# Rows of experts 1 to 7 gathered as column strips and transposed by VectorE, and the first x by ScalarE's queue

## The chip, the cores and the metric

One core of one Trainium2 chip. The metric is device time in microseconds (us) of one execution: the median of three runs of the kernel before is 932.55 us (932.34 to 934.09). Tensors are fp32. TensorE (PE) multiplies, VectorE (DVE) and ScalarE (ACT) work on SBUF and PSUM, GpSimd (POOL) issues the indirect DMAs (gathers and scatters through a list of row numbers), and SyncE (SP) issues most of the plain DMAs.

## What is computed

```python
xc = einsum('bsd,bdh->bsh', x, W[cat_ids]) + b[cat_ids][:, None, :]   # x: (4, 1024, 512)
xf = xc.reshape(4096, 512)
probs = softmax(xf @ Wr); eidx = argmax(probs)                        # 8 experts
rank = position of the token among those of its expert
keep = rank < 512                                                     # capacity 512
xe = xf[dispatch]                                                     # (8, 512, 512)
h = maximum(einsum('ecd,edf->ecf', xe, W1), 0)                        # F = 2048
ye = einsum('ecf,efd->ecd', h, W2) * (p_tok of the token, 0 if not kept)
out = x + scatter-add of ye to its tokens
```

Four batches each pick one of 64 weight matrices, a router sends each token to one expert, each expert takes at most 512 tokens, and a two-layer ReLU network of the expert is added to x.

## The kernel before

**First stage (0 to about 147 us): the conditional linear layer and the router.** x is loaded in eight chunks of 512 tokens (`load_x`, L245; the first in four DMAs), and each chunk is turned on TensorE against an identity (`transpose_x`, L265, PSUM to SBUF by ScalarE at L274). Every large product in this kernel is done in seven block products in place of eight, with sums and differences of blocks made by VectorE beforehand; `linear` (L470) issues one of the seven at L488 and evicts with VectorE (`finish`, L516; `plus_bias`, L501), and `done` (L509) stores a 256 KB piece of the result into DRAM, in two tensors `xc0_dram` and `xc1_dram` that hold the left and the right 256 columns of each token. Rank and expert give each token a slot; `rank` (L441) scatters (probability, token number) into the DRAM table `slots` with eight indirect DMAs for each batch (L460). `load_w1` (L174) loads the 1 MB of expert weights of one group g of the hidden units, as two halves of 512 KB (L179), and `sum_w1` makes their sums.

**Junction.** ScalarE's queue reads `slots` back as `table` (L637), GpSimd turns it into `src_row` and `dst_row` (L644), the row numbers that gathers and scatters use.

**Experts (from about 147 us, some 96 us each).** `gather` (L682) issues the indirect DMAs at L691. For expert e, `xg` (four buffers of 128 tokens x 512) takes the rows of `xc0_dram` and `xc1_dram`, eight gathers of 1 KB rows; `xr` (four buffers) takes the rows of x, the residual, four gathers of 2 KB rows. `fetch(e)` (L698) copies 8 columns of `src_row` into a tile `at` by VectorE, and then issues both: the residual of expert e and the rows of expert e+1. It is called from `between` at g = 1 and held behind VectorE's latest work. `transpose_rows` (L707) turns a tile of 128 tokens on TensorE (L719: four transposes of 128x128), evicts it into `xe` (L720; VectorE for expert 0, else ScalarE), and behind the last tile VectorE makes the block sums of `xe` (L729 to L733). `first_layer` (L740) issues the products at L746 and evicts into `h`; `second_layer` (L795) the products at L803, `inner_product` (L851) those at L856, where four of the seven second-layer products are themselves split in seven, with their blocks' sums from `inner_sums` (L815, at L160 to L170). `add` (L787) multiplies a result by the probability and adds it onto the residual rows (L791), and four scatters (L889) write these to the output. x itself is copied to the output by three DMAs from DRAM to DRAM (L920).

**Order.** TensorE and SP run in the order of the program (`manual_schedule`). VectorE, ScalarE and GpSimd are put in order by a planner when the kernel is built: what is ready, by place in the program, with `high_priority` ahead. The stretch that ends an expert is the part of the program around the change:

```python
            second_layer(e, 6)
            inner_sums(e, 5)
            ahead(0)
            small(*[(2, q) for q in (1, 5, 2, 6, 3, 7)])
            ahead(1, 2)
            small((2, 4))
            inner_sums(e, 3)
            second_layer(e, 7)
            inner_sums(e, 4)
            small((5, 5), (5, 2))
            ahead(3)
            small(...)
```

`ahead(c)` is `transpose_rows(e + 1, c)`. PSUM results of `first_layer`, `second_layer` and `inner_product` share two buffers each of three tags x, y, z.

Of the kernel before, what the change touches and what calls it, by code (L numbers as in the profile page):

```python
# [8 lines left out]
F32 = mybir.dt.float32  # L9
I32 = mybir.dt.int32  # L10
AF = mybir.ActivationFunctionType
ALU = mybir.AluOpType
# [4 lines left out]
P = 128  # L17

FAR = 8192.0
# [3 lines left out]
def kernel(  # L23
# [11 lines left out]
    nc = tc.nc  # L35
    B, S, D = x.shape
    NCAT = cond_w.shape[0]
    E, _, F = w1.shape
    T = B * S
    CAP = -(-T // E)  # L40
    KC = D // P
# [4 lines left out]
    HT = CT // 2  # L46
    SC = CAP // P
    HK = KC // 2
# [3 lines left out]
    NG = F // (2 * HB * P)  # L52
    W1G = 3
    NS = E * SC
    Q = 32
    ROW = 2
    xf = x.rearrange("b s d -> (b s) d")
# [7 lines left out]
    def keep_warm(pool, n):  # L65

        ps = pool.tile([P, D], F32, tag="t", name="ps_idle")
        for _ in range(n):
            nc.tensor.matmul(ps, lhsT=idle[:, 0:P], rhs=idle, start=True, stop=True)
# [13 lines left out]
    def unordered(group, ins):  # L83
# [10 lines left out]
    nc.vector.memset(idle, 0.0)  # L94
    wr_sb = const.tile([P, KC, Q], F32, name="wr_sb")
    nc.vector.memset(wr_sb, 0.0)
    nc.scalar.dma_start(
        out=wr_sb[:, :, 0:E], in_=wr.rearrange("(kc p) e -> p kc e", p=P)
    )
    zeros = const.tile([P, T * ROW // P], F32, name="zeros")  # L100
    nc.vector.memset(zeros, 0.0)
    slots = dram.tile([T, ROW], F32, name="slots")
    nc.scalar.dma_start(out=slots.rearrange("(p s) r -> p (s r)", p=P), in_=zeros)
    before = const.tile([P, P], F32, name="before")
    make_upper_triangular(nc, before, diag=False)
    ones = const.tile([P, P], F32, name="ones")
# [22 lines left out]
        nc.vector.memset(t, 0.0)  # L129


    xc_dram = [dram.tile([T, HD], F32, name=f"xc{j}_dram") for j in range(2)]

    table = const.tile([P, SC, E, ROW], F32, name="table")
    src_row = const.tile([P, NS], I32, name="src_row")
    dst_row = const.tile([P, NS], I32, name="dst_row")


# [35 lines left out]
    def load_w1(e, g):  # L174

        t = w1p.tile([P, 7, HK, HB * P], F32, tag="w1", name=f"w1_{e}_{g}")
        for half in range(2):
            f = half * F // 2 + g * HB * P
            nc.sync.dma_start(  # L179
                out=t[:, 2 * half : 2 * half + 2, :, :].rearrange("p a k f -> p (a k) f"),  # L180
                in_=w1[e, :, f : f + HB * P].rearrange("(k p) f -> p k f", p=P),
            )
        w1s[e, g] = t

    def sum_w1(e, g):
# [3 lines left out]
    with (  # L189
# [52 lines left out]
            nc.vector.tensor_tensor(t3, b22, b12, ALU.subtract)  # L242
            nc.vector.tensor_tensor(t4, b21, t2, ALU.subtract)

        def load_x(c):  # L245
            t = xin.tile([P, XT, D], F32, tag="x", name=f"x_{c}")
            n = 1 if c == 0 else XT
            for j in range(0, XT, n):
                nc.sync.dma_start(
                    out=t[:, j : j + n, :],  # L250
                    in_=xf[c * CT + j * P : c * CT + (j + n) * P, :].rearrange(
                        "(j p) d -> p j d", p=P
                    ),
                )
            xrows[c] = t
# [214 lines left out]
        def linear(b, g, k):  # L470
# [15 lines left out]
            for j in range(2):  # L486
                for kc in range(HK):
# [10 lines left out]
                        skip_group_check=True,  # L498
                    )

            def plus_bias(into, half):  # L501
                return nc.vector.tensor_tensor(
                    into,
                    ps,
                    bias[:, half * HD : (half + 1) * HD].unsqueeze(1).to_broadcast([P, 2, HD]),
                    ALU.add,
                )

            def done(t, i, j):  # L509
                at = c * CT + i * HT  # L510
                nc.sync.dma_start(
                    out=xc_dram[j][at : at + HT, :].rearrange("(j p) d -> p j d", p=P),
                    in_=t,
                )

            def finish():  # L516
                if k in (1, 6, 7):
                    if (b, k) == (LATE, 6):
                        banks[key, k] = late["all"][:, g, :].rearrange("p (j d) -> p j d", d=HD)
                    else:  # L520
                        banks[key, k] = parts.tile(
                            [P, 2, HD], F32, tag=f"s{k}", bufs=2, name=f"s{k}_{b}_{g}"
                        )
                    evicted = plus_bias(banks[key, k], 0 if k == 1 else 1)
                    if k == 1:
                        latest[0] = evicted
                if k in (2, 3):
                    t = banks.pop((key, 1 if k == 2 else 6))
                    latest[0] = nc.vector.tensor_tensor(t, ps, t, ALU.add)
                    done(t, 0, int(k == 3))  # L530
                if k == (7 if b < B - 1 else 5):
                    t = banks.pop((key, 7))
                    nc.vector.tensor_tensor(t, banks[key, "y"], t, ALU.add)
                    done(t, 1, 1)
                    if b == LATE:
                        t = banks[key, 6]
                        nc.vector.tensor_tensor(t, banks[key, "y"], t, ALU.add)
                if k == 4:
                    t = parts.tile([P, 2, HD], F32, tag="c", bufs=2, name=f"xc10_{c}")
                    plus_bias(t, 0)  # L540
                    done(t, 1, 0)
# [77 lines left out]
        }  # L619

        with tc.manual_schedule(engines={mybir.EngineType.PE, mybir.EngineType.SP}):
            load_x(0)
            load_batch(0)
            load_x(1)
            load_batch(1)
            load_x(2)
            load_batch(2)
            keep_warm(ps_t, 3)
            for i in range(XT):
                transpose_x(0, i)  # L630
            for b in range(B):
                for i, product in enumerate(ORDERS[b]):
                    linear(*(b, *product)[-3:])
                    for f, *at in loads.get((b, i), []) + beside.get((b, i), []):
                        f(*at)
# [20 lines left out]
    ps_p = ctx.enter_context(tc.tile_pool(name="ps_p", bufs=2, space=PSUM, reuse_waits="tile"))  # L656

    rows, residual, xes, hs = {}, {}, {}, {}

    def load_w2(e, when=None):  # L660

# [20 lines left out]
    def gather(e, pool, sources, into, at):  # L682

        n = D // len(sources)
        for j, source in enumerate(sources):
            for c in range(SC):
# [8 lines left out]
                    in_offset=bass.IndirectOffsetOnAxis(ap=at[:, c : c + 1], axis=0),  # L695
                )

    def fetch(e):  # L698

        at = rowp.tile([P, 2 * SC], I32, tag="at", name=f"at_{e}")  # L700
        n = min(2 * SC, NS - e * SC)
        nc.vector.tensor_copy(at[:, 0:n], src_row[:, e * SC : e * SC + n])  # L702
        gather(e, xr, [xf], residual, at[:, 0:SC])
        if e + 1 < E:
            gather(e + 1, xg, xc_dram, rows, at[:, SC : 2 * SC])

    def transpose_rows(e, c, parts=range(2)):  # L707

        if e not in xes:
            xes[e] = xep.tile([P, 7, HK, HC * P], F32, tag="xe", name=f"xe_{e}")  # L710

        t = xes[e]
        r = rows[e * SC + c]
        half, at = divmod(c, HC)
        n = len(parts)
        lo = parts[0] * HK
        ps = ps_e.tile([P, KC, P], F32, tag="t", name=f"ps_e_{e}_{c}_{lo}")
        for kc in range(n * HK):
            nc.tensor.transpose(ps[:, kc, :], r[:, (lo + kc) * P : (lo + kc + 1) * P], ident)  # L719
        (nc.vector.tensor_copy if e == 0 else nc.scalar.copy)(  # L720
            t[
                :, 2 * half + parts[0] : 2 * half + parts[0] + n, :, at * P : (at + 1) * P
            ].rearrange("p b k n -> p (b k) n"),
            ps[:, 0 : n * HK, :],
        )
        if c == SC - 1:
            b11, b21, b12, b22, t1, t2, t4 = (t[:, k, :, :] for k in range(7))
            if 0 in parts:
                nc.vector.tensor_tensor(t1, b12, b11, ALU.subtract)  # L729
            if 1 in parts:  # L730
                nc.vector.tensor_tensor(t2, b22, t1, ALU.subtract)
                nc.vector.tensor_tensor(b12, b22, b12, ALU.subtract)
                nc.vector.tensor_tensor(t4, b21, t2, ALU.subtract)  # L733


    LEFT = {1: 0, 2: 1, 3: 6, 4: 3, 5: 4, 6: 5, 7: 2}
# [184 lines left out]

    with tc.manual_schedule(engines={mybir.EngineType.PE, mybir.EngineType.SP}):
        gather(0, xg, xc_dram, rows, src_row)

        for part, half, then in (
            ([0], 0, [(0, 1)]),
            ([0], 1, [(1, 1), (0, 5), (1, 5)]),
            ([1], 0, [(0, 2)]),
            ([1], 1, [(1, 2)]),
        ):  # L930
            for c in range(half * HC, (half + 1) * HC):
                transpose_rows(0, c, part)
            for g, k in then:
                first_layer(0, g, k)

        load_w2(0, xes[0][:, 3, 0, HC * P - 1 :])
        for e in range(E):
            for g in range(NG):
                if e == 0 and g < 2:
# [21 lines left out]
                for k, q in turns:  # L961
                    inner_product(e, k, q)

            def ahead(*tiles):
                for c in tiles:
                    if e + 1 < E:
                        transpose_rows(e + 1, c)

            second_layer(e, 6)
            inner_sums(e, 5)  # L970
            ahead(0)
            small(*[(2, q) for q in (1, 5, 2, 6, 3, 7)])
            ahead(1, 2)
            small((2, 4))
            inner_sums(e, 3)
            second_layer(e, 7)
            inner_sums(e, 4)
            small((5, 5), (5, 2))
            ahead(3)
            small(  # L980
                *[(5, 1), (5, 3), (5, 6), (3, 5), (5, 7), (3, 2), (5, 4), (3, 1)],
                *[(4, 5), (4, 1), (3, 6), (4, 2), (4, 6)],
# [35 lines left out]
```

## Time and profile before

| what | value |
|---|---|
| three runs, us | 934.09, 932.34, 932.55 |
| the profiled execution's own time, us | 930.86 |
| its span in the profile, us | 929.1 |
| granted TensorE clock | 0.998 |
| DMA | 123.32 MB, mean 133 GB/s |
| gathers of 1 KB rows (L691) | 64 of 0.96 to 1.04 us |
| gathers of residual rows (L691) | 32 of 1.41 us |
| transposes of expert rows (L719) | 128 of 273 ns |

A line of the timeline or of the groups names engine, line of the kernel, operation, and out<-in by the program's names. In the timeline the first number is the start and the second the time from the first start to the last end, both in us, and a bracket tells how long the engine had been idle and what ended that. PEld is the weight load ahead of a product. Matmuls overlap, so the distance from one group's start to the next is their price, not their duration.

### The profile page before, as it was taken

To read this page: it belongs to the slowest core of one execution; us is meant where nothing else is said; L and a number is where in the kernel's file an instruction comes from. 1 tells how busy PE (TensorE), PEld (TensorE's weight loads), DVE (VectorE), ACT (ScalarE), POOL (GpSimd) and SP (SyncE) were. 2 spreads that over 40 slices of the span, in tenths; PEclk is the share of its full clock that TensorE was granted. 3 is DMA by queue.
4 is the path that set the end of the run, shared out by engine and by line. 5 is a ranking of instruction groups with operands and counts; after the bars stand their busy time and mean duration, and the time that the engine had idled before them with its cause. 6 is when DMAs were issued, how large, how long until landed. Compare 5 with 4: busy or idle time off the path is not lost.

```text
span 929.1 us, 13272 instructions
## 1 busy us (share of the span) xinstructions
PE 915.9 (99%) x5318; PEld 817.5 (88%) x5318; DVE 654.9 (70%) x1222; ACT 193.5 (21%) x350; POOL 181.7 (20%) x173
## 2 busy tenths in 40 slices
PE   9999999999999999999999999999999999999996
PEld 6788787889988998899889988999889988998886
DVE  4656684589549954987488847883789368945793
ACT  3323200321132103210331023112311132113200
POOL 0043443060141013201230024001500150012001
PEclk9999999999999999999999999999999999999999
DMA  8475223992372118310841085106520562044001
GB/s 299 157 242 167 81 80 117 343 379 90 100 254 100 46 61 266 127 47 21 275 152 46 1 277 164 58 1 227 182 91 2 202 202 90 2 154 159 1 1 46
DMA packets 95727, 123.32 MB, mean 133 GB/s; under 512 B 8516, under 2 KB 83268, under 8 KB 95474
## 3 DMA queue, kind: packets, MB, share of 16 engines
q1 hardware_dynamic: 85634, 97.54, 31.5%
q0 software_dynamic: 9216, 24.85, 8.1%
q8 instruction: 42, 0.69, 0.3%
q10 hardware_dynamic: 816, 0.08, 0.1%
q14 instruction: 19, 0.16, 0.1%
HBM read 105.96 MB, written 25.23 MB: 141 GB/s over the span
## 4 chain that ended last, share of the span: by engine, by line
PE 64%; issue 18%; DVE 13%; POOL 3%; DMA 1%; ACT 0%; POOLq 0%; DVEq 0%
PE hx L746 19%; PE hy L746 9%; PE yx L856 7%; PE xcx_lin L488 6%; PE hz L746 5%; PE yx L803 4%; PE yy L856 3%; DVE rows L791 2%; PE xcy_lin L488 2%; POOL rows L691 2%; DVE h L160 2%; DVE h L161 2%; PE ps_xT L273 1%; PE xcz_lin L488 1%; DVE h L163 1%
## 5 line engine op out<-in xcount | busy, mean ns | idle before, releaser
L746 PE MATMUL hx<-xe,w 128*128 128x256 f32 x1024 | 237.7, 379 | 1.2 <-DVE xe L720 1.0
L746 PEld LDWEIGHTS hx<-xe,w 128*128 128x128 f32 x1024 | 193.8, 190 | 27.7 <-DVE xe L720 1.2
L889 POOL DMA_INDIRECT out_dram<-rows,dst_row x32 | 32.0, 999 | 465.3 <-DVE rows L791 428.6
L746 PE MATMUL hy<-xe,w 128*128 128x256 f32 x512 | 120.6, 379 | 0.0
L803 PE MATMUL yx<-w_b,h 128*128 128x256 f32 x512 | 113.1, 379 | 0.0
L746 PEld LDWEIGHTS hy<-xe,w 128*128 128x128 f32 x512 | 97.3, 190 | 13.2
L803 PEld LDWEIGHTS yx<-w_b,h 128*128 128x128 f32 x512 | 96.7, 190 | 12.8
L761 ACT COPY s<-hx 128x512 f32<-128x512 f32 x96 | 55.8, 582 | 222.7 <-PE hx L746 222.7
L765 DVE TENSOR_TENSOR h<-hy,s 128x512 f32<-128x512 f32 x64 | 44.1, 688 | 76.0 <-PE hy L746 51.7
L766 ACT ACTIVATE h<-h 128x512 f32<-128x512 f32 x96 | 60.5, 630 | 150.7 <-DVE h L765 150.7
L856 PE MATMUL yx<-w_b,h 128*128 128x128 f32 x640 | 83.4, 275 | 0.7 <-DVE rows L791 0.6
L791 DVE SCALAR_TENSOR_TENSOR rows<-yx,table,rows 128x128 f32<-128x128 f32 (+1 forms) x160 | 59.9, 398 | 30.8 <-PE yx L856 30.7
L856 PEld LDWEIGHTS yx<-w_b,h 128*128 128x128 f32 x640 | 77.3, 192 | 1.1 <-DVE rows L791 1.0
L691 POOL DMA_INDIRECT rows<-in_x_dram,at x32 | 45.2, 1412 | 145.4 <-DVE at L702 106.2
L691 POOL DMA_INDIRECT rows<-xc_dram,at x56 | 58.4, 1043 | 21.4 <-issue 14.3
L746 PE MATMUL hz<-xe,w 128*128 128x256 f32 x256 | 60.6, 379 | 0.6 <-DVE xe L720 0.6
L765 DVE TENSOR_TENSOR h<-hz,s 128x512 f32<-128x512 f32 x32 | 22.0, 688 | 55.4 <-PE hz L746 55.4
L803 PE MATMUL yx<-w_t,h 128*128 128x256 f32 x256 | 56.6, 379 | 0.0
L460 POOL DMA_INDIRECT slots<-row,dest x32 | 36.3, 1136 | 96.4 <-DVE dest L456 87.9
L746 PEld LDWEIGHTS hz<-xe,w 128*128 128x128 f32 x256 | 48.5, 190 | 7.4 <-DVE xe L720 0.9
L803 PEld LDWEIGHTS yx<-w_t,h 128*128 128x128 f32 x256 | 48.6, 190 | 6.6
L856 PE MATMUL yx<-w_t,h 128*128 128x128 f32 x384 | 52.1, 279 | 0.4
(160 smaller groups left out, 1244.3 us busy)
## 6 DMA issues: line engine op xcount, KB each, us to landing
w<-in_L_ffn_W_dram SPq DMA_DIRECT2D x64, 512.0 KB, 4.3
w_b<-in_L_ffn_W_dram SPq DMA_DIRECT2D x32, 1024.0 KB, 10.9
x<-in_x_dram SPq DMA_DIRECT2D x7, 1024.0 KB, 8.7
xc_dram<-s SPq DMA_DIRECT2D x22, 256.0 KB, 2.7
out_dram<-in_x_dram SPq DMA_DIRECT2D x2, 2816.0 KB, 20.3
cw<-in_L_cond_W_dram SPq DMA_DIRECT2D x3, 1024.0 KB, 10.6
out_dram<-in_x_dram SPq DMA_DIRECT2D x1, 2560.0 KB, 12.2
xc_dram<-xc SPq DMA_DIRECT2D x8, 256.0 KB, 2.3
```

Of the source, the lines that this page charges most:

```text
L160: eng.tensor_tensor(s1, a21, a22, ALU.add)
L460: nc.gpsimd.indirect_dma_start(out=slots, out_offset=bass.IndirectOffsetOnAxis(ap=dest[:, j : j + 1], axis=0), in_=row[:, j, :], in_offset ...
L488: nc.tensor.matmul(ps[:, j, :], lhsT=left[:, kc, j * P : (j + 1) * P], rhs=right[k][:, kc, :], start=((k in OPENS or (b, k) == (LATE, 3)) ...
L691: nc.gpsimd.indirect_dma_start(out=into[e * SC + c][:, j * n : (j + 1) * n], out_offset=None, in_=source, in_offset=bass.IndirectOffsetOnA ...
L746: nc.tensor.matmul(ps[:, j, :], lhsT=w1s[e, g][:, LEFT[k], kc, j * P : (j + 1) * P], rhs=xes[e][:, RIGHT1[k], kc, :], start=(k in OPENS an ...
L761: nc.scalar.copy(banks[key, k], ps)
L765: latest[0] = nc.vector.tensor_tensor(into, ps, part, ALU.add)
L766: nc.scalar.activation(into, into, AF.Relu)
L791: nc.vector.scalar_tensor_tensor(row, ps, table[:, half * HC + at, e, 0:1], row, ALU.mult, ALU.add)
L803: nc.tensor.matmul(ps[:, at, :], lhsT=hs[e][:, m // HB, LEFT[k], m % HB, at * P : (at + 1) * P], rhs=w2s[e][RIGHT2[k]][:, m, :], start=(k ...
L856: nc.tensor.matmul(ps, lhsT=left[:, g, :], rhs=right[:, g, :], start=(q in OPENS and g == 0), stop=(q == LAST[BANK[q]] and g == NG - 1), s ...
L889: nc.gpsimd.indirect_dma_start(out=of, out_offset=bass.IndirectOffsetOnAxis(ap=dst_row[:, n : n + 1], axis=0), in_=residual.pop(n), in_off ...
```

## The change

- `done` stores each row of 256 columns as four strips of 64 in another order of columns: strip b holds the columns 32b to 32b+31 of the first 128 and those of the second. The evictions write their tile in that order (`strip`, `bank_of`); the stored pieces become 256 bytes.
- For experts 1 to 7 `gather_strips` reads strips in place of rows: 32 gathers of 128 strips of 256 bytes for each expert, the partition block b of the target taking strip b of 32 tokens. The strip numbers are made once, by four loads of `slots` on ScalarE's queue and eight GpSimd operations (`strip_rows`), and read in place. `turn_strips` turns a 128x512 tile on VectorE in blocks of 32x32, straight into `xe`. The strips of expert 1 are asked for ahead of the loop over experts, those of e+2 when e+1 has been turned. `fetch` keeps the residual alone.
- Expert 0 keeps its gathers and its transposes on TensorE; since its columns come in the new order, its first-layer weights are loaded in that order of rows, 16 DMAs for each g in place of 2.
- The first chunk of x is issued by ScalarE's queue, and the router weights' load and the clearing of `slots` behind it; `keep_warm` multiplies twice in place of three times.

```diff
+    strip_at = const.tile([P, 1], F32, name="strip_at")
+    for b in range(VB):
+        nc.gpsimd.memset(strip_at[b * V : (b + 1) * V, :], float(b))
...
+            into = t[:, 2 * half : 2 * half + 2, :, :]
+            if e > 0:
...
+            rows_of = w1[e, :, f : f + HB * P].rearrange(
+                "(a k q b c) f -> b k c a q f", a=2, k=HK, b=2, c=V
+            )
+            for b in range(2):
+                for k in range(HK):
+                    lo = (b * HK + k) * V
+                    for a in range(2):
+                        nc.sync.dma_start(out=into[lo : lo + V, a], in_=rows_of[b, k, :, a])
...
+            def strip(t):
+                return t.rearrange("p j d -> p (j d)").rearrange(
+                    "p (b j k c) -> p j k b c", b=VB, j=2, c=V
+                )
+
+            def bank_of(t):
+                return t.rearrange("p j (k b c) -> p j k b c", b=VB, c=V)
...
+                return nc.vector.tensor_tensor(strip(into), bank_of(ps), bank_of(added), ALU.add)
...
-                    out=xc_dram[j][at : at + HT, :].rearrange("(j p) d -> p j d", p=P),
-                    in_=t,
+                    out=xc_dram[j][at : at + HT, :].rearrange(
+                        "(j p) (b d) -> p b j d", p=P, b=VB
+                    ),
...
-            load_x(0)
+            load_x(0, nc.scalar)
             load_batch(0)
+            nc.scalar.dma_start(
+                out=wr_sb[:, :, 0:E], in_=wr.rearrange("(kc p) e -> p kc e", p=P)
+            )
+            nc.scalar.dma_start(out=slots.rearrange("(p s) r -> p (s r)", p=P), in_=zeros)
...
-            keep_warm(ps_t, 3)
+            keep_warm(ps_t, 2)
...
+    def strip_rows():
+        for b in range(VB):
+            nc.scalar.dma_start(
+                out=strips[b * V : (b + 1) * V].rearrange("r a c e w -> r a (c e w)"),
+                in_=slots.rearrange("(a r s) w -> r a (s w)", a=VB, r=V),
+            )
+        into = src_strip.rearrange("p e (c a) -> p e c a", a=VB)
+        for a in range(VB):
+            row = strips[:, a, :, :, 1].rearrange("p c e -> p e c")
+            nc.gpsimd.tensor_scalar(row, row, FAR, float(T - 1), ALU.add, ALU.min)
+            nc.gpsimd.tensor_scalar(
+                into[:, :, :, a], row, float(VB), strip_at, ALU.mult, ALU.add
+            )
...
+    def gather_strips(e):
+        at = src_strip[:, e, :]
+        for half in range(2):
+            for j in range(2):
+                t = xg.tile([P, D], F32, tag="rows", name=f"strips_{e}_{half}_{j}")
+                n = D // (HC * VB)
+                for q in range(HC * VB):
+                    c = half * HC * VB + q
+                    nc.gpsimd.indirect_dma_start(
+                        out=t[:, q * n : (q + 1) * n],
+                        out_offset=None,
+                        in_=xc_dram[j].rearrange("t (b d) -> (t b) d", b=VB),
+                        in_offset=bass.IndirectOffsetOnAxis(ap=at[:, c : c + 1], axis=0),
+                    )
+                rows[e, half, j] = t
...
+        at = rowp.tile([P, SC], I32, tag="at", name=f"at_{e}")
+        nc.vector.tensor_copy(at, src_row[:, e * SC : (e + 1) * SC])
+        gather(e, xr, [xf], residual, at)
...
+    def turn_strips(e, half, j):
+        t = rows.pop((e, half, j)).rearrange("p (q k c) -> p k q c", k=HK, c=V)
+        into = xe_of(e)[:, 2 * half + j, :, :].rearrange("p k (q r) -> p k q r", r=V)
+        nc.vector.transpose(into, t)
...
         gather(0, xg, xc_dram, rows, src_row)
+        strip_rows()
...
         load_w2(0, xes[0][:, 3, 0, HC * P - 1 :])
+        gather_strips(1)
         for e in range(E):
...
-            ahead(0)
             small(*[(2, q) for q in (1, 5, 2, 6, 3, 7)])
-            ahead(1, 2)
+            if e + 1 < E:
+                for half in range(2):
+                    for j in range(2):
+                        turn_strips(e + 1, half, j)
+            if e + 2 < E:
+                gather_strips(e + 2)
             small((2, 4))
...
-            ahead(3)
+            if e + 1 < E:
+                sum_xe(e + 1)
```

## The prediction

> **What bounds the kernel now.** I read the page first: its span, its busy shares and the shares of the chain that ended last.
>
> ```profile
> span 929.1 us, 13272 instructions
> ...
> PE 915.9 (99%) x5318; PEld 817.5 (88%) x5318; DVE 654.9 (70%) x1222; ACT 193.5 (21%) x350; POOL 181.7 (20%) x173
> ...
> PE 64%; issue 18%; DVE 13%; POOL 3%; DMA 1%; ACT 0%; POOLq 0%; DVEq 0%
> ```
>
> TensorE is busy for 99% at a granted clock of 9 in all 40 slices. The kernel is as long as TensorE's list of work plus its few waits, so each part is priced by what it takes from that list and by which wait it adds. Then the timeline of the stretch that ends expert 1, for the transposes (L719), the next product (L856) and VectorE's sums beside them:
>
> ```profile
> 316.37 1.04 PE L719 MATMUL ps_e<-ident,rows 128*128 128x128 f32 x8
> 316.61 0.34 DVE L791 SCALAR_TENSOR_TENSOR rows<-yx,table,rows 128x128 f32<-128x128 f32 x1
> 316.87 0.68 DVE L170 TENSOR_TENSOR w_t<-w_t,w_t 128x512 f32<-128x512 f32 x1
> ...
> 317.24 1.06 PE L856 MATMUL yx<-w_b,h 128*128 128x128 f32 x8
> 317.47 0.68 DVE L160 TENSOR_TENSOR h<-h 128x512 f32<-128x512 f32 x1
> 318.07 0.68 DVE L167 TENSOR_TENSOR w_b<-w_b 128x512 f32<-128x512 f32 x1
> ...
> 326.82 0.60 PE L719 MATMUL ps_e<-ident,rows 128*128 128x128 f32 x4
> ...
> 327.26 1.06 PE L856 MATMUL yx<-w_t,h 128*128 128x128 f32 x8
> ...
> 330.25 1.06 PE L856 MATMUL yy<-w_b,h 128*128 128x128 f32 x8
> ```
>
> The transposes' price is the distance to the next product (317.24 - 316.37 = 0.87 for eight), not their mean of 273 ns, which overlaps. VectorE runs back to back here, but ahead of need: the first sums for product k=3 (L160, L167) end at 318.75, and TensorE uses them at 330.25.
>
> Last, the same view around expert 0's first corner sum, where VectorE, GpSimd and TensorE meet:
>
> ```profile
> 174.20 0.92 SPq L179 DMA_DIRECT2D w<-in_L_ffn_W_dram  x2
> ...
> 189.77 3.23 POOL L691 DMA_INDIRECT rows<-in_x_dram,at  x1 [0.30 <-issue]
> ...
> 190.97 1.21 DVE L168 TENSOR_TENSOR w_t<-w_b,w_t 128x1024 f32<-128x1024 f32 x1
> ...
> 196.78 1.02 POOL L691 DMA_INDIRECT rows<-in_x_dram,at  x1 [0.30 <-issue]
> ...
> 203.74 0.87 DVE L791 SCALAR_TENSOR_TENSOR rows<-yx,table,rows 128x256 f32<-128x256 f32 x2
> ...
> 206.82 7.07 PE L803 MATMUL yx<-w_t,h 128*128 128x256 f32 x32
> ```
>
> The gathers of the residual rows run from 187.7 to 197.8. The adds at 203.74 need two of those four tiles, and free the PSUM buffer that the product at 206.82 writes (its weights load from 206.60). There are 2.0 us between the adds' end (204.6) and that.
>
> **A. TensorE's transposes go.** Per expert: 0.43 (310.57 to 311.00) + 0.87 + 0.44 = 1.74 us of pure TensorE time. Seven experts: -12.2. Expert 0's end also loses a wait for gathered rows (213.72 to 214.80 for four, 1.08 in place of 0.43): -0.65. ScalarE's 28 copies (15.7 us) hid beside TensorE: 0.
>
> **B. VectorE's transposes come:** 28 of 128x512, absent from this trace. Nearest row: a two-input sum of that size, 0.68 us, one each 0.60 when back to back. The Trainium skill's page VectorE: DVE Perf Modes, in "Rules for kernel authors", speaks against the change: a 128x128 transpose belongs on TensorE, VectorE having 32x32 blocks alone. Its section "The three transpose paths" gives 311 ns for 128 bf16 columns; with 1.05 ns a column, the slope of L791 (348 ns for 128, 482 for 256), I estimate 311 + 384 x 1.05 = 714 ns for 512. By that rule a block costs 0.18 against TensorE's 0.11 (0.44 / 4), a loss; by the trace the 0.11 is on the bound and the 0.18 is not. Four take 2.4 to 2.9 us; k=3's sums then end near 321.5 against 330.25 - 1.74 = 328.5. Left is the wait of single evictions behind a longer backlog; before, one such wait of 0.24 us per expert shows (L81). I take 0.15 more for each of seven: +1.0 (bounds 0 and +8; a gain is excluded, since VectorE only gets work). If the cover went, all 2.9 x 7 = 20 us would show.
>
> **C. GpSimd's list.** Eight gathers of 1 KB rows per expert (L691, 1043 ns) become 32 of 256-byte strips. A gather has 128 indices either way; the scatters of 8-byte rows (L460) take 1136 ns, so the size of a row hardly counts and I keep 0.95 + 0.30 between two = 1.25 us clear, 40 us per expert of 96. From expert 1 on they run ahead of need, from about 222 on expert 0's clock; the four scatters (245 to 250) and the next residual gathers (266 to 272) wait behind them, to about 270 and 284; the adds come at 300. Cost 0; cover 15 us.
>
> Expert 0 is different. Its 32 gathers for expert 1 start when its own rows are transposed (about 157) and stand ahead of `fetch(0)` in the program, which I take for GpSimd's order. From 157 to 178 VectorE is mostly idle: 16 gathers at 1.27. From 178 to 200.8 VectorE is back to back. The skill's page SBUF — State Buffer, section "SBUF: two separate sides", says that a GpSimd operation that reads SBUF (here its indices) and a VectorE operation with two SBUF inputs exclude each other for a whole instruction. The row above agrees: the 3.23 us gather ends 0.9 after VectorE's next one-SBUF-input operation (192.11). By the rule taken strictly each gather costs 3.2 + 0.3 there. By the rows, the 14 gathers that ran in such stretches average 1.49 + 0.30 = 1.79; I take that: 13 more, 29 by 200.8, all 32 by 204.6, the second residual gather issued by 207.3. Its packets then share the DMA engines with the third out-copy (packets of 45 KB, 1.7 us each in the packet records), which before landed at 192.6 + 19.3 = 211.9. The strips move the same bytes as the old gathers, only earlier, so I keep that end: rows at 212.0, between 207.3 + 3 and 206.0 + 10.7 (what gathers at 203 to 206 took to land). Adds end at 212.9 where 206.6 was needed: **+6.3** (bounds 0 and +18). Behind the adds on VectorE stand the inner sums, but they shift with TensorE.
>
> **D. Start.** The warm-up ends about 1.8 us earlier (6 passes in 5.49 us become 4), x no longer holds SP until 2.95, so `cond_w` (3.99) and the bias behind it go about 1.0 earlier; ScalarE issues x from about 0.7 in place of 1.14, and its two loads that follow are needed late. The first product (9.44) could gain 1.7, but the bias, awaited at 12.18 (L502), gains only SP's 1.0 and holds VectorE's next sums, and with them the third product. -1.0 (bounds -1.7 and +0.5, if the two rings share badly).
>
> **E. Stores and the junction.** 32 stores go from 1 KB to 256-byte pieces. Packet records: 46 ns for 1 KB, 18 ns for 256 bytes, so 64 x 18 - 16 x 46 = +0.4 us of DMA each. They hide except the last: the second half's gathers wait for it (5.42 us to 151.21), and the rows' cover there is 1 us or less. +0.7 (bounds 0 and +2.5). GpSimd's eight small index operations (0.36 us for the like, L644) fit in that 5.42 us wait; after it they'd delay the strips by 3.
>
> **F. SP.** 16 issues for each of four w1 tiles, near 0.45 us (four x issues in 1.81), 7.2 in place of 1.07. In the first stage stores move by up to 4 us; their buffers are double and nobody waits: 0 (bounds 0 and +1). At 174.2 the out-copies move 6 us later, counted in C. The strided evictions keep their size (0.69): 0 (to +1).
>
> **Sum:** -12.2 - 0.65 + 1.0 + 6.3 - 1.0 + 0.7 = -5.85. The profiled execution took 930.86 us, span 929.1 plus 1.8 around it, and becomes 925.0. It lay 1.7 below the median of 932.55, to which I apply the same difference: **926.7**.
>
> **The rivals.** *The residual rows come much later (slower).* Place: GpSimd, 178 to 200.8. At the strict 3.5 us only 6 or 7 gathers fit, the 32 end near 212.7, the second residual gather at 215.4, its rows at 218 to 226. With 222 the stall is 16.3, net +4.2: 936.7. It decides when the rows land after 217.9, where stall equals gain (12.15). For it: the 3.23 and 3.17 us rows, in just that stretch. Against: 12 of the 14 took 1.75 or less. Chance 0.26.
> *No stall.* The residual gathers get ahead, by the scheduler's order or because the strips are done by 200: -12.15, 920.4. For it: 1.25 us is by far the commonest spacing. Against: 32 of those alone reach 197. Chance 0.22.
> *VectorE becomes the bound.* If a transpose costs what a 128x1024 sum does (1.22), four add 4.9 us and evictions wait an operation longer, 1.2 per expert, 8.4 in place of 1.0: 934.1. For it: VectorE has no gap from 305 to 333. Against: about 9 us of lead. Chance 0.10.
> *Likeliest,* as summed: 0.42.
>
> **The numbers.** About 0.2% (1.9 us) is what a measurement of this kernel can tell from no change. Faster: 0.36 of the likeliest, 0.22, and 0.02 of the others, 0.60. Same: 0.06 + 0.05 + 0.02 = 0.13. Slower: 0.21 of the first rival, 0.06 of the third, 0.27. Range 918.5 (no stall, the whole 1.7 at the start) to 939 (rows near 224).
>
> **What would show it.** No L719 transposes past expert 0, and periods of 94.5 us in place of 96.2 between the later experts' scatters: A. VectorE's transposes near 0.65 us: B. A gap in TensorE before the second `second_layer` product of expert 0, ended by VectorE's L791 adds, those by a DMA of residual rows: C; no gap means the second rival, one over 12 us the first. First product near 7.8, third near 13.6: D. I am wrong altogether if a gap shows before each expert's first corner sum: then the 15 us of cover in C is gone, six times over.

## The result and the profile after

The changed kernel takes 1109.78 us (four runs, 1107.76 to 1112.31) against 932.44 us: a ratio of 1.190 (95% interval 1.187 to 1.193). The forecast was 926.7. Side by side on another chip later: 1112.77 against 932.68, ratio 1.194 (1.191 to 1.196).

The page of the profiled run (1108.86 us): span, busy shares, three of the rows of 40 slices, and the chain that ended last.

```profile
span 1107.1 us, 13382 instructions
...
PE 950.8 (86%) x5204; PEld 838.5 (76%) x5204; DVE 670.4 (61%) x1250; ACT 177.7 (16%) x322; POOL 346.5 (31%) x353
...
PE   9999995596699849985999659984999579999997
...
POOL 0243457326310731147111723065113711001101
PEclk9999997698799869996899869986999779999999
...
PE 51%; another core or an unknown queue 21%; issue 19%; POOL 4%; DVE 3%; DMA 1%; ACT 1%; POOLq 0%; DVEq 0%
```

Before, TensorE had 9 in every slice but the last, and its clock had 9 in all. Now it has seven hollows, each beside a 6 or 7 of GpSimd: these are the trains of strips (a train is a run of gathers, one after the other). The clock falls with the idle time. DVE's share of the chain, 13% before, is 3%, and in its place stands a releaser that the profile can't name.

The chain around the train for expert 3 (gathers from 360.11 to 401.67), in order of time:

```profile
358.53 0.70 DVE h L835
359.24 0.02 issue
359.26 0.63 ACT h L836
359.89 45.66 another core or an unknown queue
405.55 0.02 issue
405.58 0.27 ACT p L947
405.89 2.07 PE yy L926 x8
```

And the busy time of the engines there (columns: stretch, its length, PE, PEld, DVE, ACT, POOL, clock, share of DMA, GB/s):

```profile
355.00:360.00 5.00, 5.00 (x25) 4.41 (x24) 4.39 (x9) 1.23 (x2) 0.00 (x0) 1.00 0.05 17
360.00:365.00 5.00, 5.00 (x25) 4.40 (x24) 5.00 (x9) 0.00 (x0) 3.84 (x4) 1.00 0.65 212
...
370.00:375.00 5.00, 1.16 (x8) 0.97 (x8) 1.90 (x4) 0.00 (x0) 3.81 (x4) 1.00 0.12 26
...
395.00:400.00 5.00, 0.37 (x1) 0.26 (x1) 0.00 (x0) 0.00 (x0) 3.78 (x5) 0.50 0.12 28
400.00:405.00 5.00, 0.00 (x0) 0.00 (x0) 0.00 (x0) 0.00 (x0) 1.36 (x2) 0.50 0.06 16
405.00:410.00 5.00, 4.07 (x17) 3.78 (x18) 4.26 (x9) 0.70 (x3) 0.00 (x0) 0.50 0.00 0
```

GpSimd goes on steadily, one gather each 1.25 us for the most part. About eight gathers in, TensorE stumbles; it works again for some time (5.00 of 5 us from 380 to 385), and from 395 on TensorE, VectorE and ScalarE stand still until some 4 us after the last gather. ScalarE waits 45.7 us for something that the profile can't name ("another core or an unknown queue", "remote" in the timeline). The timeline of the end of this gap:

```profile
391.43 0.38 PE L926 MATMUL yx<-w_t,h 128*128 128x128 f32 x2 [1.84 <-issue]
...
392.85 0.37 PE L926 MATMUL yx<-w_t,h 128*128 128x128 f32 x1 [1.04 <-issue]
...
394.26 0.57 PE L926 MATMUL yx<-w_t,h 128*128 128x128 f32 x1 [1.04 <-issue]
...
405.49 1.66 DVE L861 SCALAR_TENSOR_TENSOR rows<-yx,table,rows 128x256 f32<-128x256 f32 x4 [19.01 <-remote]
```

These products belong to one group of eight. They wait for no result ("issue"), and yet start 1.4 us apart, where the whole group takes 0.9 us before. So it is not only that results of other engines come late. It is no lack of DMA either: the DMA engines are busy for 6 to 12% there. Nor is it the loading of instructions: from 370 to 405 the only packets are those of the gathers (queue and kind, packets, MB, share).

```profile
q0 software_dynamic: 832, 0.85, 11.1%
```

From one expert's first product to the next's, experts 1 to 5 take 120.5 to 122.3 us where it was 96.2. Experts 6 and 7, with no train beside them, start 94.8 apart. Against 94.8, and 98.2 for expert 0 (99.6 less the 1.4 of an expert), that is 133.5 + 57.4 = 190.9 us lost in seven trains, 27 each. Less 1.4 won at the start, 7 x 1.4 on the experts and 1.5 behind the last product, it makes 178.2; the spans lie 178.0 apart.

### The profile page after: what moved, and what is told of

Same layout as the page of the kernel before. It is cut to its first block, busy times and chain, and to the rows that moved or that the text cites. A ratio compares the mean times of both kernels' runs of the same rounds, so it can differ in the third digit from the quotient of the medians.

```text
span 1107.1 us, 13382 instructions
## 1 busy us (share of the span) xinstructions
PE 950.8 (86%) x5204; PEld 838.5 (76%) x5204; DVE 670.4 (61%) x1250; ACT 177.7 (16%) x322; POOL 346.5 (31%) x353
## 4 chain that ended last, share of the span: by engine, by line
PE 51%; another core or an unknown queue 21%; issue 19%; POOL 4%; DVE 3%; DMA 1%; ACT 1%; POOLq 0%; DVEq 0%
PE hx L816 14%; PE hy L816 7%; PE yx L926 5%; PE xcx_lin L502 5%; PE yx L873 4%; PE hz L816 3%; POOL strips L754 3%; PE yy L926 3%; PE xcy_lin L502 2%; PE ps_xT L287 1%; PE xcz_lin L502 1%; POOL out_dram L959 1%; PE yz L926 1%; PE ps_lT L393 1%
## 5 line engine op out<-in xcount | busy, mean ns | idle before, releaser
L754 POOL DMA_INDIRECT strips<-xc_dram,src_strip x224 | 223.0, 996 | 256.5 <-DVE xe L788 190.4
L873 PE MATMUL yx<-w_b,h 128*128 128x256 f32 x512 | 123.7, 404 | 0.0
L873 PEld LDWEIGHTS yx<-w_b,h 128*128 128x128 f32 x512 | 104.8, 206 | 15.8
L926 PE MATMUL yx<-w_b,h 128*128 128x128 f32 x640 | 91.4, 291 | 29.5 <-issue 24.3
L926 PEld LDWEIGHTS yx<-w_b,h 128*128 128x128 f32 x640 | 83.8, 204 | 32.9 <-issue 25.5
L816 PEld LDWEIGHTS hy<-xe,w 128*128 128x128 f32 x512 | 97.6, 191 | 13.4
L926 PE MATMUL yx<-w_t,h 128*128 128x128 f32 x384 | 66.4, 309 | 45.7 <-issue 34.9
L926 PEld LDWEIGHTS yx<-w_t,h 128*128 128x128 f32 x384 | 56.8, 218 | 50.1 <-issue 37.8
L738 POOL DMA_INDIRECT rows<-in_x_dram,at x32 | 40.1, 1254 | 132.1 <-DVE at L765 123.2
L926 PE MATMUL yy<-w_t,h 128*128 128x128 f32 x192 | 30.4, 309 | 43.9 <-ACT p L947 43.9
L926 PEld LDWEIGHTS yy<-w_t,h 128*128 128x128 f32 x192 | 28.0, 220 | 48.0 <-ACT p L947 47.6
```

Of the source, the lines that this page charges most:

```text
L738: nc.gpsimd.indirect_dma_start(out=into[e * SC + c][:, j * n : (j + 1) * n], out_offset=None, in_=source, in_offset=bass.IndirectOffsetOnA ...
L754: nc.gpsimd.indirect_dma_start(out=t[:, q * n : (q + 1) * n], out_offset=None, in_=xc_dram[j].rearrange("t (b d) -> (t b) d", b=VB), in_of ...
L816: nc.tensor.matmul(ps[:, j, :], lhsT=w1s[e, g][:, LEFT[k], kc, j * P : (j + 1) * P], rhs=xes[e][:, RIGHT1[k], kc, :], start=(k in OPENS an ...
L873: nc.tensor.matmul(ps[:, at, :], lhsT=hs[e][:, m // HB, LEFT[k], m % HB, at * P : (at + 1) * P], rhs=w2s[e][RIGHT2[k]][:, m, :], start=(k ...
L926: nc.tensor.matmul(ps, lhsT=left[:, g, :], rhs=right[:, g, :], start=(q in OPENS and g == 0), stop=(q == LAST[BANK[q]] and g == NG - 1), s ...
```

## The experiments

Theories: LENGTH (a close run of gathers holds the other engines up, whatever the rest), SIZE (pieces of 256 bytes do it), INDEX (indices read in place do it). A fourth, CHIP, came late. The first eight runs were on one chip, the next four on a second, then four on a third, the last two on a fourth. "Period" is the distance from an expert's first product to the next's. Runs 1 to 9 and 12 to 16 were timed once each; the kernel before varied between 930.55 and 935.30 us in 19 runs.

**1. Long rows in a long train** (kernel before):

```diff
             gather(e + 1, xg, xc_dram, rows, at[:, SC : 2 * SC])
+            for again in range(3):
+                for j, source in enumerate(xc_dram):
+                    for c in range(SC):
+                        nc.gpsimd.indirect_dma_start(
+                            out=rows[(e + 1) * SC + c][:, j * HD : (j + 1) * HD],
...
```

> The kernel before, with each gather of 1 KB rows for the next expert made four times into the same place (the same rows again, the result unchanged): one train of 4 + 32 gathers behind each fetch, in place of 4 + 8. Theory LENGTH (an unbroken train of some ten or more gathers holds up the other engines, whatever a piece's size): each train of about 46 us stalls TensorE as the train of 32 strips does, some 20 to 30 us for each of seven experts, 1070 to 1140 us. Theory SIZE (pieces of 256 bytes do it) and theory INDEX (indices read in place, 64 bytes or more apart, from the large table do it): no stall, 931 to 938 us, since the extra gathers lie in GpSimd's idle time. A train of 36 without a stall would refute LENGTH.

1079.13 us against 932.49. A train that starts at 409.24, whose rows are needed some 45 us later, holds TensorE up after 26 us (columns as above):

```profile
435.00:440.00 5.00, 0.18 (x1) 0.00 (x0) 2.86 (x4) 0.63 (x1) 3.96 (x4) 0.84 0.55 122
```

So SIZE and INDEX fall as the only cause. But the total doesn't measure the hold-up: a train of 50 us also ends later than its rows are needed, and run 12 shows that such lateness alone can cost as much.

**2. Bursts of eight**, each behind a copy of its indices (`gather_strips` now takes half and j, and is called from `between`):

```diff
+        if e + 1 < E:
+            behind(gather_strips, e + 1, *divmod(g, 2))
```

> The changed kernel, with the 32 strip gathers of an expert in four bursts of 8, one for each g of the expert before, each behind a small copy of its 8 index columns by VectorE that is held behind VectorE's latest work; so bursts of about 10 us begin some 13 to 20 us apart. LENGTH: no burst reaches the point (about the eighth gather) from which the engines stood still, so the stalls go: 915 to 930 us. SIZE: every burst holds the others up for about its length, so most of the stall stays, above 1030 us. INDEX: the copied indices alone cure it, 915 to 930 us; the next kernel tells that from LENGTH.

985.40 us, between all forecasts. The bursts did not stay apart: the residual's four gathers joined the second, and the third and fourth ran together, 8, 12 and 16 in a row 3 to 9 us apart. Periods of experts 1 to 6: 100.9 to 103.1.

**3. Indices copied**, the train as it was:

```diff
+        at = rowp.tile([P, SC * VB], I32, tag="ats", name=f"ats_{e}")
+        nc.vector.tensor_copy(at, src_strip[:, e, :])
```

> The changed kernel, with the 32 index columns of an expert copied by VectorE into a small tile ahead of the train, which stays one train of 32 strips. INDEX: no stall, 915 to 930 us. LENGTH and SIZE: as the changed kernel, 1095 to 1115 us.

1110.94 us. INDEX is out.

**4. A pause behind each gather:**

```diff
+                    for _ in range(2):
+                        with tc.issue_after(last[0].ins):
+                            last[0] = nc.gpsimd.memset(idle, 0.0)
```

> The changed kernel, with two clears of a 128x512 tile by GpSimd (about 0.5 us each, estimated from its 128x128 clears of 0.2 us) behind every strip gather, so that a train keeps its 32 strips and its indices read in place but goes at some 2.3 us a gather in place of 1.25 (about 75 us of an expert's 95). If it is the rate of a train that fills something up (LENGTH in its form of a backlog), the stalls go or shrink by far: 920 to 960 us, with perhaps some waits for late strips. SIZE with each piece costing the same whatever the pace, and INDEX: 1095 us or more, with the other engines held up through the whole longer train.

948.81 us. Experts 2 to 6 take 94.8 to 94.9 us: with pauses the hold-up is gone, with the same 32 strips and indices. The loss is in experts 0 and 1 (116.0 and 106.1), whose strips and residual rows now come late.

**5. One clear per gather, and expert 0's residual rows first** (runs 7, 8, 9 and 14 build on this one):

```diff
+                    for _ in range(1):
+                        with tc.issue_after(last[0].ins):
+                            last[0] = nc.gpsimd.memset(idle, 0.0)
...
+        with tc.issue_after(last[0].ins):
+            fetch(0)
         gather_strips(1)
```

> The changed kernel, with one clear of a 128x512 tile by GpSimd (0.54 us) behind every strip gather, so an even pace of about 1.8 us, and with expert 0's residual rows asked for ahead of expert 1's strips. Measured so far: at 2.3 us experts take 94.8 us each, the stall is gone; at 1.25 us it costs 26 us an expert. If what counts is that GpSimd breaks off between two gathers, or a rate limit that lies between 1.25 and 1.8: experts 2 to 7 take 94.8 us, and with expert 1's strips a few us late the whole is 918 to 930 us. If the limit lies above 1.8 us: 5 to 15 us more for each expert, 950 to 1020 us.

919.77 us, periods of 94.8 from expert 1 on. Its GpSimd, then its busy time beside a train:

```profile
440.19 0.95 POOL L757 DMA_INDIRECT strips<-xc_dram,src_strip  x1 [0.16 <-issue]
441.14 0.54 POOL L765 MEMSET idle<- 128x512 f32 x1
441.84 1.09 POOL L757 DMA_INDIRECT strips<-xc_dram,src_strip  x1 [0.16 <-issue]
```

```profile
445.00:450.00 5.00, 5.00 (x25) 4.41 (x24) 1.24 (x2) 1.69 (x3) 4.51 (x7) 1.00 1.10 336
450.00:455.00 5.00, 5.00 (x24) 4.39 (x24) 2.31 (x6) 2.30 (x4) 4.51 (x7) 1.00 0.48 114
```

One gather each 1.65 us for the most part (1.76 in the mean) in place of 1.25, and TensorE is full.

**6. Rows twice** (run 1 with `range(1)`): trains of 4 + 16.

> The kernel before, with each gather of 1 KB rows made twice in place of four times: trains of 4 + 16 gathers. If a train of long rows stalls from about its 24th gather on, as the trains of 36 did: no stall, 931 to 936 us. If all above some 10 to 12 gathers costs its own length: 8 gathers beyond, some 10 us for each of seven experts, about 1000 us.

972.92 us, periods of 98.5 to 102.5 for experts 1 to 6: long rows are held up too, in a train that is over 28 us after its start, long before its rows are needed. Expert 0 (108.1) and the end behind the last product are longer as well, but so they are in run 13, which has no hold-up.

**7 and 8. Eights and fours:** nine clears behind every eighth gather; two clears behind every fourth.

> As the even pace, but eight strip gathers back to back at 1.25 us and then nine clears (4.9 us): the same mean rate as the even pace of 1.8 us. A backlog that drains in a pause: no stall or a small one, 918 to 935 us, since eight back to back were harmless so far. If each pair of back-to-back gathers costs by itself, or the pause of 4.9 us is too short to drain what eight left: 5 to 15 us more for each expert, 950 to 1020 us.

> As the even pace, but four strip gathers back to back and then two clears (1.1 us): a mean of 1.55 us, so that expert 1's strips come in time. If any short break suffices: 916 to 922 us, the prediction's sum with the residual rows in time and no stall. If the mean rate decides and 1.55 us is too quick: between the even pace and the changed kernel, 950 to 1060 us.

964.85 and 930.41 us. Eights at a mean of 1.85 us cost some 8 us per expert (periods of experts 1 to 5: 100.1 to 106.2, mean 103.0), fours at a mean of 1.57 about 2 (96.4 to 97.6). So no limit on the mean rate, since the even pace of run 5 (1.76) costs nothing and the slower eights do: what counts is how many come 1.25 us apart. Four cost 2 / 8 = 0.25 us, eight 8 / 4 = 2, thirty-two 27.

**9. A tick for a pause** (`memset(idle[:, 0:1], 0.0)`):

> As the even pace, but GpSimd clears a single column (0.10 us) in place of 512 (0.54 us) between two strip gathers, so the pace is about 1.3 us. If it is enough that another instruction stands between two gathers: as the even pace, 918 to 922 us. If it is time that is needed after every gather (0.3 us of sequencer time and 0.54 us of clearing were enough, 0.3 us alone were not): stalls come back, 20 us an expert or nearly so, 1000 to 1110 us.

1120.23 us. The 0.11 us clear hid in the 0.30 us that passes between two gathers anyway, so the distance stayed 1.25. An instruction between them is not enough; distance is.

**10. The even pace again,** on the second chip:

> The even pace once more (one clear of 0.54 us behind every strip gather, expert 0's residual rows ahead of expert 1's strips), for an interval: 919 to 921 us, a ratio of 0.985 to 0.988 to the kernel before.

920.03 us (919.97 to 920.53) against 931.99: ratio 0.9866 (0.9846 to 0.9887). It lies 1.1 to 1.5% under the kernel before. With run 9 beside it on the same chip, differing in the length of the clear alone, this is the plainest evidence for distance.

**11. The start alone** (the diff's `load_x(0, nc.scalar)`, the two loads behind it, and `keep_warm(ps_t, 2)`, on the kernel before):

> The kernel before with the start of the change alone: the first chunk of x by ScalarE's queue, the router weights and the clearing of slots behind it, two warm-up products in place of three. The prediction's part D, priced by itself: 1.0 us less (bounds 1.7 less and 0.5 more), about 931.5 us. In the changed kernel the first product of expert 0 came 1.4 us earlier, with the stores' change in it; if that is all D's, 931.1 us.

931.07 against 931.99: ratio 0.9988 (0.9976 to 0.9999).

**12. Long rows four times, with pauses** (run 1 with a clear behind each gather):

> The kernel before with each gather of 1 KB rows made four times, as in the first experiment (1079 us), but with one clear of 0.54 us behind every gather from expert 1's rows on. If unbroken runs of gathers are the cause, whatever the rest of the change: the stalls go, 931 to 936 us, though it moves 22 MB more than the kernel before. If the extra gathers cost by their number or their bytes: 1000 us or more still.

1082.59 us: the expectation missed, for a reason that the waits tell (engine, line, what it waited for, us in all, times, longest).

```profile
PEld ps_e L739 <- DMA rows<-xc_dram,at: 138.1, 14, 30.3
```

The train of 65 us ends later than TensorE needs the rows: an ordinary wait with its DMA named, 138.1 us over seven trains. In the expert from 402 to 519 it is 16.9 of the 19.7 us by which the expert grew, in two waits, and the clock falls in them. Up to there TensorE's semaphore updates (the marks that tell other engines of a finished product) come on time, as far as they are recorded. The train was too long to test the theory; the theory did not fall by it.

**13 and 14. The same with rows twice; half the pause:**

> The kernel before with each gather of 1 KB rows made twice (972.9 us without a pause) and a clear of 0.54 us behind every gather from expert 1's on: 20 gathers in some 36 us, and the rows are needed 45 us after the train's start, so that nothing can come late, as it did where they were made four times with pauses (TensorE waited 19.7 us per expert for rows there). HOLD-UP by gathers that follow one another too closely: the stalls go, 931 to 936 us. If long rows stall the engines in spite of pauses: 960 to 980 us.

> The even pace with half the pause: a clear of 256 columns (about 0.33 us) behind every strip gather, so one every 1.44 us in place of 1.65 (no stall) and 1.25 (26 us an expert). If the hold-up is a backlog with a sharp limit of rate between 1.25 and 1.65 us, this shows on which side 1.44 lies: 918 to 921 us, or, if above the limit, a stall of a few us to 10 us for each expert, 940 to 990 us.

947.66 us, outside both ranges: experts 1 to 6 have periods of 96.2 to 96.5, so no hold-up, but expert 0 is 12.5 us longer (112.1, rows late again) and the end behind the last product 4.2. And 919.71 us, periods of 94.8 to 94.9. By themselves both seem to speak for distance. But:

**15 and 16. Extra loads that nobody waits for** (kernel before, behind each expert's 12 gathers, 24 loads of 128 x 256 bytes into an unused tile: plain, or indirect as here):

```diff
+            for q in range(24):
+                lo = q % 8 * (D // 8)
+                with tc.issue_after(last[0].ins):
+                    last[0] = nc.gpsimd.indirect_dma_start(
+                        out=idle[:, lo : lo + D // 8],
...
```

> The kernel before, with 24 plain loads of 128 pieces of 256 bytes by GpSimd's queue behind each expert's 12 gathers, into a tile that nobody reads (extra work, the result unchanged); nobody needs them, so they cannot come late. If any close run of DMAs issued by GpSimd holds the others up: 20 to 30 us for each expert as with strips, 1050 to 1110 us. If it takes an index read for every piece, or if plain loads are issued at another pace: 931 to 940 us.

> As the last, but the 24 extra loads are indirect: gathers of 128 pieces of 256 bytes, with the copied indices, into the tile that nobody reads; all else is the kernel before (no turning by VectorE, no strip stores, no new loads). HOLD-UP: 15 to 30 us for each of seven experts, 1040 to 1140 us, and the stall ends about 4 us after the last gather, though nobody waits for it. If something else in the change was needed for the stall: 931 to 940 us.

928.25 and 929.87 us: no hold-up at all, in run 16 with trains of 36 gathers, most of them 1.25 us apart (run 15's plain loads go off 0.54 us apart). LENGTH as it stood fell here. Runs 13 to 16 were on the third chip.

Run 11 (second chip) has the trains of 12 of the kernel before, and they leave a mark. TensorE's products follow one another as before, but its semaphore updates come at 273.89, 278.09 and 283.16, where in the trace of before they come every 1.73 or 3.45 us. ScalarE, which copies these products, starts one copy at 283.24, 2.4 us late. The next train shows it in ScalarE's waits for the first layer's products (360 to 392; us in all, times, longest), before and in run 11:

```profile
ACT s L761 <- PE hx L746: 9.8, 6, 2.9
...
ACT s L761 <- PE hx L746: 11.0, 5, 5.2
```

So that chip holds up 12 gathers as well, and slack hides it.

**17 and 18. The changed kernel and run 16's kernel, on one chip:**

> The changed kernel itself, once more, beside the next. The last four runs (on another chip than the twelve before them) showed no hold-up in a run of 36 gathers 1.25 us apart, and in a kernel with the trains of 12 of before, on a chip of the earlier runs, TensorE's semaphore updates were late from about the eighth gather on (a gap of 5.1 us where they come every 1.73), hidden by slack. So whether gathers hold the engines up may depend on the chip. Theory CHIP: the two kernels of this call go together: on a chip that holds up, 1105 to 1120 us here and a stall in the next; on one that does not, 915 to 928 us here (the prediction as it stood, 926.7, less what the residual rows of expert 0 gain if they are in time). Theory KERNEL (the extra gathers of the next are harmless by what they are): 1105 to 1120 us here and no stall in the next.

> The kernel before with 24 extra gathers of 256-byte pieces behind each expert's 12, once more, beside the changed kernel on the same chip. CHIP: on a chip that holds up, 15 to 30 us more for each of seven experts, 1040 to 1140 us; on one that does not, 929 to 933 us together with a changed kernel of some 920. KERNEL: 929 to 933 us beside a changed kernel of some 1110.

1112.77 us (ratio 1.1935), and 1048.11 us (three runs: 1037.35, 1048.11 and 1059.63; the two quicker give a ratio of 1.118, 1.110 to 1.126). The very kernel that took 929.87 on the third chip is held up on the fourth, with periods of 103.6 to 125.3. Both from 20 us after a train's first gather on (same columns as above); first the third chip:

```profile
286.00:291.00 5.00, 5.00 (x25) 4.41 (x24) 4.29 (x7) 2.33 (x4) 4.02 (x4) 1.00 0.35 95
291.00:296.00 5.00, 5.00 (x25) 4.41 (x24) 5.00 (x9) 1.22 (x2) 3.78 (x5) 1.00 0.49 161
```

The fourth:

```profile
306.00:311.00 5.00, 4.54 (x22) 3.67 (x21) 3.40 (x4) 1.22 (x2) 4.09 (x4) 1.00 0.11 21
311.00:316.00 5.00, 2.00 (x10) 1.44 (x9) 3.90 (x6) 1.81 (x3) 4.11 (x3) 1.00 0.53 168
```

KERNEL is refuted. The hold-up takes a close run of gathers and a chip (or something that differs with it) on which this happens; the first, second and fourth are such, and so is the one of the profile after, by its stalls. The cure by distance is shown on the first two (runs 4, 5 and 10; run 12 as far as its waits tell). Runs 13 to 15 ran where nothing is held up, so they say nothing for it: whether 1.44 us is far enough, and whether plain loads are harmless where gathers are not, stays open.

## Why the prediction was wrong, step by step

**C failed, in the sentence "Cost 0; cover 15 us"** for the gathers from expert 1 on. I asked who waits for the strips, and found them early enough; they were (32 in 41.6 us; no wait of VectorE or TensorE for a strip DMA shows). I took it as given that a busy GpSimd costs the others nothing while nobody waits for it. On these chips its gathers, 1.25 us apart, stopped all of them: 27 us per train, seven times. A gap came in each expert that has a train, though not where the text's last test looked for it, and its reading ("the 15 us of cover in C is gone") does not hold, for the gaps are no waits for strips. Nothing in the profile of before shows this: that run's chip did not hold up its 12 gathers. The nearest hint was the count, 32 in place of 12 in a row, for which no row existed. I bounded the cost of the index reads from both sides, not that of the train's length.

**C, the pace:** predicted 1.25 us clear and some 1.79 beside a busy VectorE. In the changed kernel it is 1.25 in the median and 1.31 in the mean (VectorE mostly stands still). Where nothing is held up, run 16's 168 extra gathers beside VectorE's work take 1.14 us in the mean:

```profile
L711 POOL DMA_INDIRECT idle<-xc_dram,at x168 | 190.8, 1136 | 51.2 <-issue 50.9 <-DMA idle<-xc_dram,at 0.3
```

So the strict reading of the Trainium skill's page SBUF — State Buffer ("SBUF: two separate sides"), taken as 3.2 us for each gather from the longest rows of the trace before, is not what the rows show; single gathers are long (up to 5.32 us in run 14), most are not. Expert 0's 6.3 us for late residual rows could not be seen on its own: VectorE was held up until 203.13, so the copy of the indices came at 215.78 and the second gather at 218.19 (predicted 207.3). With them issued first (runs 5 and 10) there is no such stall.

**A and B were right for experts 1 to 6.** Where nothing holds it up, such an expert takes 94.8 in place of 96.2: -1.4, predicted -1.74 + 0.15 = -1.59. VectorE's transposes take 694 ns, between the nearest row (0.68) and the estimate of 714:

```profile
L788 DVE STREAM_TRANSPOSE xe<-strips 128x512 f32<-128x512 f32 x28 | 18.9, 694 | 0.0
```

They ran between other sums, from 359.14 on, with no wait ahead of them. For expert 0 the gain (1.59 and A's 0.65) does not show: with the even pace (runs 5 and 10) it takes 100.0 to 100.2 in place of 99.6. In run 5 the pauses make expert 1's strips late there, the last gather at 221.38, and TensorE waits 1.04 us at 231.93 for VectorE, which is behind with them.

**D was right:** -0.9 us by itself (interval -2.2 to -0.1), predicted -1.0; the first and third products of the whole kernel come at 7.93 and 13.24, predicted 7.8 and 13.6. **E and F:** the first product of expert 0 comes at 147.44 in place of 148.84, and at 147.88 with D alone (run 11), so E's +0.7 does not show. F's 16 issues take 7.58 us, predicted 7.2. The kernel ends 1.5 us sooner behind its last product, which was in no step; run 16, whose products are those of the kernel before, ends as soon, so the strips are not what did it.

**The sum:** with the hold-up taken away and the residual rows in time, 919.8 and 920.0 us were measured; the rival "no stall" gave 920.4. That they agree so closely is partly luck, for errors cancel. In run 5's profile experts 1 to 6 gain 8.7 us (predicted 9.5), the start 1.6 (predicted 0.3, D less E) and the end 1.5 (predicted 0), while expert 0 loses 0.6 (predicted gain 2.2). The changed kernel itself was not run on a chip that holds nothing up, so whether 926.7 would have held there is not shown.

## What to carry to other kernels

Many small gathers are not free because nobody waits for them: before counting GpSimd as spare, see whether a profile of the same chip shows a run of that many, that close, and whether TensorE's rhythm beside it, and the waits of the others for TensorE, stay as they were. Where that can't be known, keep gathers apart (here a clear of 0.54 us behind each, 1.65 us from one to the next, cost nothing) and issue those that are needed first ahead of the train. When an experiment contradicts a theory, check first whether it ran on the same chip. Every time in this document was taken with the recording on; whether the kernel is held up without it is not shown.

## What the hardware did that I had not expected

- A run of gathers 1.25 us apart slows and then stops TensorE, VectorE and ScalarE from about the eighth on, until about 4 us after the last, with DMA engines nearly idle. SyncE is held up too: in the first train its loads for expert 0 come at 203.12 in place of 174.20, after a wait of 37.9 us that the profile can't name. Which resource they share is open.
- It depends on the chip: 1048 against 930 us for one kernel.
- On the chips that are held up, the trace also has fewer records of semaphore increments, even where nothing is late: for GpSimd's scatters from 100 to 160 us, 189 of 384 in run 11 against 384 of 384 in the trace of before and in run 16. So the same chips lose records and hold engines up, and even products that wait for no result come late. Every time here comes with recorded spans, so whether the recording takes part in the hold-up can't be told; it is the rival that stands untested.
- It makes TensorE pay twice: the granted clock falls to 0.50 in the gaps and is still 0.50 from 405 to 410, when TensorE works again.
